# A message-passing kernel: additions in PSUM, the relu shared by two engines, 101 copied groups

## The chip, the core and the metric

The kernel runs on one core of a Trainium2 chip. A core has five engines with a queue of instructions each, worked off in order: TensorE (PE: matrix products, results in the accumulator memory PSUM), VectorE (DVE), ScalarE (ACT), GpSimd (POOL, which here issues the indirect gathers) and SyncE (SP, which issues plain DMAs). Engines wait for each other by semaphores. The metric is the time of one execution on the device, in microseconds (us), and the number that counts is the median of several.

## The reference

One layer of a graph network with a residual and a layer norm: 12500 nodes of 64 features, 200000 edges of 32 features, sorted by destination.

```python
msg_in = concatenate([nodes[row], nodes[col], edge_features], axis=-1)   # 64 + 64 + 32
messages = relu(msg_in @ mW1 + mb1) @ mW2 + mb2                          # hidden 128
aggregated = segment_sum(messages, col, num_segments=12500)
upd = relu(concatenate([nodes, aggregated]) @ uW1 + ub1) @ uW2 + ub2
out = layernorm(nodes + upd)
```

All is float32. `row` is the source of an edge (random), `col` its destination (sorted).

## The kernel before

**Tables.** The product of the first weight with a concatenation is a sum of products. The kernel first writes table A, the product of every node with the source part of `mW1`, to DRAM, and table B, the same for the destination part with the bias. An edge then needs one row of A (by its source) and one of B (by its destination).

**Tiles, steps and groups.** 128 edges are a tile; 1563 tiles. A step `s` has 6 tiles (261 steps), a super-step 12 tiles, two steps. In the loop over steps, `gather` (L209) has POOL fetch 128 rows of A by an indirect DMA, one instruction a tile, into one of 9 row buffers. `edge_part` (L367) has PE multiply the edge features and a one-hot of the destination within a window of 32 nodes with the edge weights and the rows of B, into a PSUM accumulator `pc` of two banks. `node_part` adds the gathered rows: DVE writes `h = pc + xg` (L394, 128x768), ACT then applies the relu to `h` in place (L395). `collect` (L424, L427) has PE sum the hidden rows `h` into the nodes of the window with a one-hot `sel`, written by DVE in `select` (L235, L237, L243) once a super-step, in even steps. `collect(s - 1)` and `edge_part(s + 1)` are issued in step s. Every 7 or 8 steps a period of nodes is closed (L441, L442), updated (L464 to L480) and normed (L486 to L510). The first ten steps gather rows of x and multiply them on PE, since A is not there yet.

**Copied groups.** In 96 of the steps (16, 19, 21, 24, ..., two in five), POOL gathers only 4 of the 6 tiles. The rows of the last two come from a copy of x that lies transposed in SBUF (`xtop`, `xbot`): for each of 128 columns an instruction copies one column for each of two tiles at once into `xc`, and PE multiplies `xc` with the weight (L370) into the same accumulator. Of the 128 columns, ACT copies 64 (`singly`, L338) and DVE 64 (`joined`, L345). In such a step the addition is 128x512 (L390) with its relu (L391), and the relu of the copied tiles reads PSUM (L392). Where a column lies comes from the edge's source number: `addresses` (L315) loads a chunk of up to 8 columns, two addresses each, from the list `col_a` into registers of the engine, and the copies behind it use them. `portion(s, total, unit)` says which columns of which group are due in step s; two copy buffers hold the groups under way.

**Order.** The order of each queue is the order of the Python loop over steps, written by hand: node part, a third or a half of DVE's copies, the norm stages of an older period, `collect(s - 1)`, `select` of the next super-step with a third of the copies between its operations, a chunk of table B (until step 50), the update, `edge_part(s + 1)`, the rest of DVE's copies, and last ACT's copies. The last lines of the loop body:

```python
            rest(s)
            joined(s, 2 if j == 0 and g + 1 < NSUP else 1, 3 if j == 0 and g + 1 < NSUP else 2)
            singly(s, 0, 1)
```

A buffer of gathered rows is free again once the addition of its step is done; `pc` (two buffers, shared with the products of table B, the update and the residual) once the last reader is done.

Of the kernel before, what the change touches and what calls it, by code (L numbers as in the profile page):

```python
# [24 lines left out]
SUB = 6  # L25
SUP = 12
NSUP = -(-NT // SUP)
NTP = NSUP * SUP
EPAD = NTP * P
NSUB = -(-NT // SUB)  # L30
# [39 lines left out]
XBASE = 8320  # L70
U8 = mybir.dt.uint8
YBASE = XBASE + 4 * XCOLS
FIRST, GAPS = 16, (3, 2)
COPIED = []
while FIRST + sum(GAPS) * (len(COPIED) // len(GAPS)) + sum(GAPS[:len(COPIED) % len(GAPS)]) < NSUB - 6:
    COPIED.append(FIRST + sum(GAPS) * (len(COPIED) // len(GAPS)) + sum(GAPS[:len(COPIED) % len(GAPS)]))
RNDS = -(-len(COPIED) // len(GAPS))
LAST = 4 * (N - 1)
ACTS, CHUNK = 64, 8


def updates():
# [19 lines left out]
def gnn_kernel(ctx: ExitStack, tc: tile.TileContext, x1T, x, eT, e_rows, src, src_row, dst, dst_row, wlist, wrow, wnext, whalf,  # L102
# [24 lines left out]
    nc = tc.nc  # L127
    const = ctx.enter_context(tc.tile_pool(name="const", bufs=1))
# [12 lines left out]
    wint = const.tile([1, len(LISTS)], I32, name="wint")  # L141
    past = const.tile([1, 1], F32, name="past")

    cols = const.tile([RNDS * len(GAPS), 2 * P], I32, name="cols")
    col_a = const.tile([RNDS * len(GAPS), P, 2], I32, name="col_a")
    w1b = const.tile([P, DH], F32, name="w1b")
    b1 = const.tile([P, DH], F32, name="b1")

# [43 lines left out]
    def tiles(s):  # L192
        return range(s * SUB, min((s + 1) * SUB, NT))
# [20 lines left out]
    with tc.tile_pool(name="sup", bufs=2) as sup, tc.tile_pool(name="work", bufs=2) as work, tc.manual_schedule():  # L214
# [13 lines left out]
        def select(g, at=None):  # L228


            nt = min(SUP, NT - g * SUP)
            l = L[g]
            c = WIN + SUP // 2 * (g % 2)
            node = cps[:, c:c + SUP // 2]
            nc.vector.tensor_scalar(node, wh[:, g * SUP // 2:(g + 1) * SUP // 2], pidx, None, op0=ALU.add)  # L235
            for r in ([slice(0, P)] if g > 2 else [slice(q, q + WIN) for q in SK]):
                nc.vector.tensor_tensor(l[r], l[r].bitcast(I32),  # L237
                                        node[r].unsqueeze(2).broadcast_to([r.stop - r.start, SUP // 2, P]),
                                        op=ALU.is_equal)
            if at is not None:  # L240
                joined(at, 1, 3)
            s = sup.tile([P, SUP, WIN], F32, name="sel")
            nc.vector.tensor_tensor(s[:, :nt], slot.unsqueeze(1).broadcast_to([P, nt, WIN]),  # L243
                                    drc[:, g * SUP:g * SUP + nt].unsqueeze(2).broadcast_to([P, nt, WIN]),
                                    op=ALU.is_equal)
            S[g] = s

        def counts(g):

            SB[g] = S[g].bitcast(BF).rearrange("p k (w h) -> p k w h", h=2)  # L250
# [36 lines left out]

        def columns_list():

            for r in range(len(GAPS)):  # L290
                v = src_row[:, ((FIRST + sum(GAPS[:r])) * SUB + SUB - 2) * P:]
                nc.sync.dma_start(cols[r * RNDS:(r + 1) * RNDS],
                                  bass.AP(v.tensor, v.offset, [[sum(GAPS) * SUB * P, RNDS], [1, 2 * P]]))
            cv = cols.rearrange("k (b e) -> k b e", b=2)
            for b, base in enumerate((XBASE, YBASE)):
                nc.vector.tensor_scalar(col_a[:, :, b], cv[:, b], 4.0, float(base), op0=ALU.mult, op1=ALU.add)

        x8, y8 = xtop.bitcast(U8), xbot.bitcast(U8)

        def portion(s, total, unit):  # L300

            rate, found = sum(GAPS) / len(GAPS), []
            begin = min(c - 2 - (j + 1) * rate for j, c in enumerate(COPIED[:len(GAPS)]))
            for j, c in enumerate(COPIED):
                lo, hi = (min(-(-int(total * (s + d - begin - j * rate) / rate * 16 + 0.5) // (16 * unit)) * unit, total) for d in (0, 1))
                lo = max(lo, 0)
                if lo < hi:
                    if c not in xc:
                        xc[c] = work.tile([P, P], F32, name="xc")
                    found.append((xc[c], j % len(GAPS) * RNDS + j // len(GAPS), lo, hi))  # L310
            return found

        def addresses(k, a, m, engine):

            _, v = nc.values_load_multi_w_load_instructions(  # L315
                col_a.rearrange("k e b -> k (e b)")[k:k + 1, 2 * a:2 * m], engines=[engine], min_val=XBASE,
                max_val=YBASE + LAST, skip_runtime_bounds_check_because="sources are node numbers")
            v = [w.with_bounds(min_val=base, max_val=base + LAST, guaranteed_mod_val=0, out_of_modulus=4)
                 for w, base in zip(v, (XBASE, YBASE) * (m - a))]
            return [(e, x8[:, bass.ds(v[2 * (e - a)] - XBASE, 4)], y8[:, bass.ds(v[2 * (e - a) + 1] - YBASE, 4)])  # L320
                    for e in range(a, m)]

        def share(todo, part, of):

            n = -(-len(todo) // of)
            todo = todo[part * n:part * n + n]
            while todo:
                o, k, a = todo[0]
                m = min(len([t for t in todo if t[1] == k]), CHUNK // 2)
                todo = todo[m:]  # L330
                yield o, k, a, a + 2 * m

        def singly(s, part, of):

            todo = [(o, k, e) for o, k, lo, hi in portion(s, ACTS, 2) for e in range(lo, hi, 2)]
            for o, k, a, m in share(todo, part, of):
                for e, top, bot in addresses(k, a, m, ET.Activation):
                    nc.scalar.activation(o[:, e:e + 1], top.bitcast(F32), AF.Identity, bias=bot.bitcast(F32))  # L338

        def joined(s, part, of):  # L340

            todo = [(o, k, ACTS + e) for o, k, lo, hi in portion(s, P - ACTS, 2) for e in range(lo, hi, 2)]
            for o, k, a, m in share(todo, part, of):
                for e, top, bot in addresses(k, a, m, ET.DVE):
                    nc.vector.tensor_tensor(o[:, e:e + 1].bitcast(I32), top.bitcast(I32), bot.bitcast(I32),  # L345
                                            op=ALU.bitwise_or)
# [26 lines left out]
        def node_part(s):  # L373

            n = len(tiles(s))
            pc = pcs.pop(s)
            h = work.tile([P, 2, SUB // 2, DH], F32, name="h")
            if s < XG:
                xt = xs.pop(s)
                for i in range(n):  # L380
                    k, b = divmod(i, 2)
                    q = 64 * b
                    nc.tensor.matmul(pc[:, b, k, :], xt[q:q + 64, k, :], w1a[q:q + 64], start=False,
                                     stop=i + 2 >= n)
                nc.scalar.activation(h, pc, AF.Relu)
            else:
                a = xg.pop(s)[0].rearrange("p (b k) f -> p b k f", b=2)
                if s in COPIED:
                    m = SUB // 2 - 1
                    nc.vector.tensor_tensor(h[:, :, :m], pc[:, :, :m], a[:, :, :m], op=ALU.add)  # L390
                    nc.scalar.activation(h[:, :, :m], h[:, :, :m], AF.Relu)  # L391
                    nc.scalar.activation(h[:, :, m:], pc[:, :, m:], AF.Relu)  # L392
                for b, m in parts(n) if s not in COPIED else []:
                    nc.vector.tensor_tensor(h[:, b, :m], pc[:, b, :m], a[:, b, :m], op=ALU.add)  # L394
                    nc.scalar.activation(h[:, b, :m], h[:, b, :m], AF.Relu)  # L395
            hs[s] = h

        def opened(u):
# [354 lines left out]
        for s in range(last + 2):  # L753
            g, j = divmod(s, SUP // SUB)
# [20 lines left out]
                    stage(K - 2)  # L775
            if s < NSUB:
                node_part(s)
                joined(s, 0, 3 if j == 0 and g + 1 < NSUP else 2)
            for stage, n in ((evacuate, 2), (statistics, 3), (deviation, 4), (norm, 5)):
                if earlier(n) is not None:  # L780
                    stage(earlier(n))
# [42 lines left out]
    with tc.If(flag > 0), tc.tile_pool(name="gen", bufs=1) as up:  # L824
# [28 lines left out]
        with tc.For_i(0, NT, 1) as t:  # L853
# [26 lines left out]
            pc = psum.tile([P, DH], F32, name="pcg", tag="pc")  # L880
# [4 lines left out]
            h = up.tile([P, DH], F32, name="hg")  # L885
# [6 lines left out]
            m = up.tile([P, 1], F32, name="m")  # L892
# [22 lines left out]
        with tc.For_i(0, NB, 1) as c:  # L915
# [24 lines left out]
            o = up.tile([P, D], F32, name="o")  # L940
# [49 lines left out]
```

## Time and profile before

| | |
|---|---|
| runs | 1737.85, 1738.25, 1740.77 us; median 1738.25 |
| profiled execution | 1741.33 us, span of the records 1739.5 us, 46406 instructions |
| POOL | 1298.0 us busy, 1371 gathers |
| ACT | 1469.7 us busy |
| DVE | 1057.8 us busy |
| PE | 1460.8 us busy, granted clock 0.579 of full speed |
| DMA | 192.43 MB, 111 GB/s over the span |

The page of the profile has the busy time of each engine, the chain of work that ended last, and groups of instructions by source line, each with its count, busy time and mean duration, and the idle time of the engine in front of it with what ended that. "Issue" means that the engine waited for nothing that the profile shows: for POOL the time to issue a gather, for DVE and ACT mostly a load of addresses, which is no busy time. A busy engine need not be the one that bounds, nor an engine with gaps be free.

### The profile page before, as it was taken

The page shows a single profiled execution, that of the slowest core. Times are in us where ns is not written, and L with a number is a line of the kernel's source. Part 1 is how long each engine was busy: PE and PEld are TensorE (multiplying, and loading weights), DVE is VectorE, ACT ScalarE, POOL GpSimd, SP SyncE. Part 2 cuts the span into 40 slices and gives each one's busy share as a digit, 9 for nine tenths or more (in the row PEclk, how much of TensorE's full clock was granted, in tenths as well). Part 3 has the DMA queues.
Part 4 walks back from the last instruction along what each step waited for, and adds up shares of the span by engine and source line. Part 5 has one row for each costly group of instructions (what it writes and reads, how often), then busy time and mean ns, then how long its engine had stood idle before and what let it go on. Part 6 is the DMA issues. An engine that isn't in the chain of part 4 may idle for free.

```text
span 1739.5 us, 46406 instructions
## 1 busy us (share of the span) xinstructions
PE 1460.8 (84%) x9620; PEld 1259.4 (72%) x9620; DVE 1057.8 (61%) x7327; ACT 1469.7 (84%) x6712; POOL 1298.0 (75%) x1380
## 2 busy tenths in 40 slices
PE   2696788888988888888987889999888878899997
PEld 2586778877777778677876777778766767777776
DVE  1527666666666666566666666666666666666642
ACT  0277989999999898899899899999999899999941
POOL 7777777777777777777777777777777777777773
PEclk8585555555555555555566555555556566565655
DMA  8773444433333333333343344343344444444442
GB/s 212 205 175 100 129 110 115 116 95 99 99 102 92 96 96 96 96 104 94 98 108 104 105 107 105 103 108 103 105 110 110 106 107 110 107 108 110 108 113 61
DMA packets 207588, 192.43 MB, mean 111 GB/s; under 512 B 57511, under 2 KB 173409, under 8 KB 207313
## 3 DMA queue, kind: packets, MB, share of 16 engines
q0 software_dynamic: 43872, 87.97, 20.6%
q1 hardware_dynamic: 148896, 92.54, 19.4%
q10 hardware_dynamic: 14546, 8.93, 1.8%
q8 instruction: 91, 1.49, 0.4%
q14 instruction: 183, 1.50, 0.3%
HBM read 171.53 MB, written 17.76 MB: 109 GB/s over the span
## 4 chain that ended last, share of the span: by engine, by line
POOL 37%; issue 23%; DMA 14%; DVE 13%; PE 8%; DVEq 3%; ACT 1%; SPq 1%; ACTq 0%; POOLq 0%
POOL xg L209 37%; DMA xg<-tab_a,src_s 10%; DVE xc L345 6%; DVE h L394 3%; PE sums L427 3%; DVEq L315 3%; PE pc L367 2%; DVE l L237 2%; DMA tab_a<-tb 1%; ACT xc L338 1%; DVE h L390 1%; PE pu L464 1%; DMA w1b<-in_mW 1%; PE pu L465 1%; PE py L478 0%
## 5 line engine op out<-in xcount | busy, mean ns | idle before, releaser
L209 POOL DMA_INDIRECT xg<-tab_a,src_s x1311 | 1239.5, 945 | 399.7 <-issue 368.6
L338 ACT ACTIVATE xc<-xtop,xbot 128x1 f32 x6144 | 1166.8, 280 | 43.0 <-issue 32.8
L345 DVE TENSOR_TENSOR xc<-xtop,xbot 128x1 int32 x6144 | 537.2, 154 | 416.4 <-issue 402.0
L427 PE MATMUL sums<-sel,h 128*128 128x32 f32 x3126 | 643.6, 373 | 21.9 <-ACT h L395 15.9
L427 PEld LDWEIGHTS sums<-sel,h 128*128 128x128 f32 x3126 | 610.0, 296 | 41.3 <-ACT h L395 17.4
L367 PE MATMUL pc<-rhs,l 64*128 64x128 f32 x3126 | 424.5, 418 | 172.3 <-DVE h L394 112.0
L367 PEld LDWEIGHTS pc<-rhs,l 64*128 64x128 f32 x3126 | 352.2, 296 | 235.6 <-DVE h L394 135.8
L395 ACT ACTIVATE h<-h 128x768 f32<-128x768 f32 x156 | 129.6, 831 | 108.8 <-DVE h L394 104.8
L394 DVE TENSOR_TENSOR h<-pc,xg 128x768 f32<-128x768 f32 x156 | 148.0, 949 | 118.5 <-DMA xg<-tab_a,src_s 76.5
L237 DVE TENSOR_TENSOR l<-l,cps 128x768 f32<-128x768 int32 (+1 forms) x134 | 127.8, 953 | 21.2 <-DMA l<-in_dst_row 16.6
L424 PEld LDWEIGHTS <-one 128*1 128x1 bf16 x1563 | 57.5, 83 | 62.4 <-issue 53.4
L424 PE MATMUL cnt<-sel,one 128*1 128x32 bf16 x1563 | 91.8, 187 | 0.9 <-issue 0.6
L390 DVE TENSOR_TENSOR h<-pc,xg 128x512 f32<-128x512 f32 x96 | 66.1, 688 | 30.2 <-PE pc L370 13.5
L243 DVE TENSOR_TENSOR sel<-cps,drc 128x384 f32<-128x384 f32 x131 | 71.6, 547 | 10.9 <-PE sums L427 10.9
L370 PE MATMUL pc<-w1a,xc 64*128 64x128 f32 x384 | 75.7, 400 | 0.0
L209 POOL DMA_INDIRECT xg<-in_x,src_s x60 | 57.4, 957 | 19.1 <-issue 17.7
L464 PE MATMUL pu<-xw,uz 128*128 128x448 f32 (+1 forms) x68 | 59.9, 982 | 13.3 <-DVE h L394 13.3
L370 PEld LDWEIGHTS pc<-w1a,xc 64*128 64x128 f32 x384 | 67.7, 315 | 0.0
L391 ACT ACTIVATE h<-h 128x512 f32<-128x512 f32 x96 | 59.3, 617 | 8.1 <-DVE h L390 7.7
L583 ACT COPY tb<-pb 128x512 f32<-128x512 f32 (+1 forms) x13 | 7.4, 569 | 59.0 <-DMA tab_a<-tb 26.8
L465 PE MATMUL pu<-sums_s,w2u 128*128 128x448 f32 (+1 forms) x68 | 53.4, 888 | 0.0
L478 PE MATMUL py<-ux,xw 128*128 128x64 f32 x268 | 49.3, 343 | 2.4 <-DVE h L394 2.4
(104 smaller groups left out, 784.8 us busy)
## 6 DMA issues: line engine op xcount, KB each, us to landing
l<-in_dst_row SPq DMA_DIRECT2D x262, 96.0 KB
l<-in_eT SPq DMA_DIRECT2D x262, 96.0 KB
xg<-tab_a,src_s POOLq DMA_INDIRECT x1311
rhs<-tab_b SPq DMA_DIRECT2D x361, 32.0 KB
tab_b<-tb SPq DMA_DIRECT2D x13, 512.0 KB
rhs<-tab_b SPq DMA_DIRECT2D x387, 16.0 KB
tab_a<-tb ACTq DMA_DIRECT2D x12, 512.0 KB
out<-y SPq DMA_DIRECT2D x33, 128.0 KB
```

The source lines that it names most:

```text
L209: nc.gpsimd.indirect_dma_start(out=a[:, i, :] if s < XG else a[:, i // 2, i % 2, :], out_offset=None, in_=A[:, :] if s >= XG else x[:, :], ...
L237: nc.vector.tensor_tensor(l[r], l[r].bitcast(I32), node[r].unsqueeze(2).broadcast_to([r.stop - r.start, SUP // 2, P]), op=ALU.is_equal)
L338: nc.scalar.activation(o[:, e:e + 1], top.bitcast(F32), AF.Identity, bias=bot.bitcast(F32))
L345: nc.vector.tensor_tensor(o[:, e:e + 1].bitcast(I32), top.bitcast(I32), bot.bitcast(I32), op=ALU.bitwise_or)
L367: nc.tensor.matmul(pc[:, b, k, :], L[g][q:q + 64, m, :], rhs[g % 2][q:q + 64, w, :], start=s >= XG or k == 0, stop=s >= XG and not copied)
L370: nc.tensor.matmul(pc[:, b, k, :], xc[s][q:q + 64], w1a[q:q + 64], start=False, stop=True)
L390: nc.vector.tensor_tensor(h[:, :, :m], pc[:, :, :m], a[:, :, :m], op=ALU.add)
L394: nc.vector.tensor_tensor(h[:, b, :m], pc[:, b, :m], a[:, b, :m], op=ALU.add)
L395: nc.scalar.activation(h[:, b, :m], h[:, b, :m], AF.Relu)
L424: nc.tensor.matmul(pn[:, bass.ds(ws[i], WIN)], one, SB[g][:, k0 + i, :, 1], start=False, stop=ends and i == n - 1)
L427: nc.tensor.matmul(ps[:, bass.ds(ws[i], WIN)], h[:, i % 2, i // 2, :], S[g][:, k0 + i, :], start=False, stop=ends and i == n - 1)
L464: nc.tensor.matmul(pu, uz, xw[u % 2][:, :n], start=True, stop=False)
```

## The change

- **Addition in PSUM.** `node_part` adds the gathered rows into `pc` in place. Then ACT applies the relu to the first bank (`h[:, 0]`, 128x384) and DVE to the second (`h[:, 1]`), both from PSUM into `h`. This holds for all full steps from the tenth on, copied or not.
- **Address loads.** The function `joined` gives way to `quota` (the columns of a step), `fetch` (load addresses for up to n columns) and `join` (copy them). A fetch of 8 columns (6 in a copied step) stands between the addition and DVE's relu, one of 4 behind the relu, one of 8 behind L237 (the select's second operation) and one of 4 behind the select's last operation. What is left goes in chunks of 8 at the end of the step.
- **Groups.** 101 groups instead of 96, at steps 16, 18, 20, 23, 25, ... 254, from a progress function: 0.43 groups a step at the start, 0.41 at the end. ACT copies 66 columns, DVE 62. Three copy buffers for two.
- **List of addresses.** `col_a` holds the addresses of the last two tiles of every step, where before it held those of the copied steps alone.

```diff
-FIRST, GAPS = 16, (3, 2)
+BEGIN, FINAL = 11, 255
+RATES = 0.43, 0.41
+SWING = 0.0
+
+def progress(s, early=0.0):
+    s = max(s + 1 - BEGIN, 0)
+    return s * (RATES[0] + (RATES[1] - RATES[0]) * s / (2 * NSUB)) + (early if s else 0.0)
+
 COPIED = []
-while FIRST + sum(GAPS) * (len(COPIED) // len(GAPS)) + sum(GAPS[:len(COPIED) % len(GAPS)]) < NSUB - 6:
-    COPIED.append(FIRST + sum(GAPS) * (len(COPIED) // len(GAPS)) + sum(GAPS[:len(COPIED) % len(GAPS)]))
+for s in range(NSUB):
+    while min(progress(s), progress(s, -SWING if s % 2 else SWING)) >= len(COPIED) + 1 and s + 3 < FINAL:
+        COPIED.append(s + 3)
-ACTS, CHUNK = 64, 8
+ACTS, CHUNK = 66, 8
...
-    cols = const.tile([RNDS * len(GAPS), 2 * P], I32, name="cols")
-    col_a = const.tile([RNDS * len(GAPS), P, 2], I32, name="col_a")
+    col_a = const.tile([P, 2, P, 2], I32, name="col_a")
...
             if at is not None:
-                joined(at, 1, 3)
+                join(fetch(quota(at), 8))
             s = sup.tile([P, SUP, WIN], F32, name="sel")
             nc.vector.tensor_tensor(s[:, :nt], slot.unsqueeze(1).broadcast_to([P, nt, WIN]),
...
             S[g] = s
+            if at is not None:
+                join(fetch(quota(at), 4))
...
-        def portion(s, total, unit):
+        def portion(s, total, early=(0.0, 0.0)):
...
-                lo, hi = (min(-(-int(total * (s + d - begin - j * rate) / rate * 16 + 0.5) // (16 * unit)) * unit, total) for d in (0, 1))
-                lo = max(lo, 0)
+                lo, hi = (min(max(int((progress(s + d, early[d + 1]) - j) * total / 2 + 1e-6) * 2, 0), total) for d in (-1, 0))
                 if lo < hi:
                     if c not in xc:
-                        xc[c] = work.tile([P, P], F32, name="xc")
+                        xc[c] = work.tile([P, P], F32, name="xc", bufs=3)
...
-        def joined(s, part, of):
-            todo = [(o, k, ACTS + e) for o, k, lo, hi in portion(s, P - ACTS, 2) for e in range(lo, hi, 2)]
-            for o, k, a, m in share(todo, part, of):
-                for e, top, bot in addresses(k, a, m, ET.DVE):
-                    nc.vector.tensor_tensor(o[:, e:e + 1].bitcast(I32), top.bitcast(I32), bot.bitcast(I32),
-                                            op=ALU.bitwise_or)
+        def quota(s):
+            if s not in quotas:
+                quotas[s] = [(o, k, ACTS + e) for o, k, lo, hi in portion(s, P - ACTS) for e in range(lo, hi, 2)]
+            return quotas[s]
+
+        def fetch(todo, n):
+            ready = []
+            while todo and n:
+                o, k, a = todo[0]
+                m = min(len([t for t in todo if t[1] == k]), n // 2)
+                del todo[:m]
+                n -= 2 * m
+                ready += [(o, *x) for x in addresses(k, a, a + 2 * m, ET.DVE)]
+            return ready
+
+        def join(ready):
+            for o, e, top, bot in ready:
+                nc.vector.tensor_tensor(o[:, e:e + 1].bitcast(I32), top.bitcast(I32), bot.bitcast(I32),
+                                        op=ALU.bitwise_or)
...
-                if s in COPIED:
-                    m = SUB // 2 - 1
-                    nc.vector.tensor_tensor(h[:, :, :m], pc[:, :, :m], a[:, :, :m], op=ALU.add)
-                    nc.scalar.activation(h[:, :, :m], h[:, :, :m], AF.Relu)
-                    nc.scalar.activation(h[:, :, m:], pc[:, :, m:], AF.Relu)
-                for b, m in parts(n) if s not in COPIED else []:
-                    nc.vector.tensor_tensor(h[:, b, :m], pc[:, b, :m], a[:, b, :m], op=ALU.add)
-                    nc.scalar.activation(h[:, b, :m], h[:, b, :m], AF.Relu)
+                m = SUB // 2 - (s in COPIED)
+                todo = quota(s)
+                if n == SUB:
+                    nc.vector.tensor_tensor(pc[:, :, :m], pc[:, :, :m], a[:, :, :m], op=ALU.add)
+                    ready = fetch(todo, 6 if s in COPIED else 8)
+                    nc.scalar.activation(h[:, 0], pc[:, 0], AF.Relu)
+                    nc.vector.tensor_scalar(h[:, 1], pc[:, 1], 0.0, None, op0=ALU.max)
+                    join(ready + fetch(todo, 4))
+                else:
+                    for b, m in parts(n):
+                        nc.vector.tensor_tensor(h[:, b, :m], pc[:, b, :m], a[:, b, :m], op=ALU.add)
+                        nc.scalar.activation(h[:, b, :m], h[:, b, :m], AF.Relu)
             hs[s] = h
...
                 node_part(s)
-                joined(s, 0, 3 if j == 0 and g + 1 < NSUP else 2)
...
             rest(s)
-            joined(s, 2 if j == 0 and g + 1 < NSUP else 1, 3 if j == 0 and g + 1 < NSUP else 2)
+            while s < NSUB and quota(s):
+                join(fetch(quota(s), CHUNK))
             singly(s, 0, 1)
```

More of the change, by code (lines that the diff above doesn't have):

```diff
@@ L72 @@
 YBASE = XBASE + 4 * XCOLS
-FIRST, GAPS = 16, (3, 2)
+BEGIN, FINAL = 11, 255
[4 more added lines that the diff above has]
+    return s * (RATES[0] + (RATES[1] - RATES[0]) * s / (2 * NSUB)) + (early if s else 0.0)
 COPIED = []
-while FIRST + sum(GAPS) * (len(COPIED) // len(GAPS)) + sum(GAPS[:len(COPIED) % len(GAPS)]) < NSUB - 6:
-    COPIED.append(FIRST + sum(GAPS) * (len(COPIED) // len(GAPS)) + sum(GAPS[:len(COPIED) % len(GAPS)]))
-RNDS = -(-len(COPIED) // len(GAPS))
+for s in range(NSUB):
+    while min(progress(s), progress(s, -SWING if s % 2 else SWING)) >= len(COPIED) + 1 and s + 3 < FINAL:
+        COPIED.append(s + 3)
 LAST = 4 * (N - 1)
-ACTS, CHUNK = 64, 8
+ACTS, CHUNK = 66, 8
 def updates():
@@ L288, in columns_list @@
         def columns_list():
[L290 to L296, printed above, removed]
+            cols = work.tile([P, 2, 2, P], I32, name="cols", tag="tb")
+            for r in range(2):
+                n = min(P, NSUB - 1 - r * P)
+                v = src_row[:, (r * P * SUB + SUB - 2) * P:]
+                nc.sync.dma_start(cols[:n, r].rearrange("k b e -> k (b e)"),
+                                  bass.AP(v.tensor, v.offset, [[SUB * P, n], [1, 2 * P]]))
+                for b, base in enumerate((XBASE, YBASE)):
+                    nc.vector.tensor_scalar(col_a[:n, r, :, b], cols[:n, r, b], 4.0, float(base), op0=ALU.mult, op1=ALU.add)
         x8, y8 = xtop.bitcast(U8), xbot.bitcast(U8)
-        def portion(s, total, unit):
-            rate, found = sum(GAPS) / len(GAPS), []
-            begin = min(c - 2 - (j + 1) * rate for j, c in enumerate(COPIED[:len(GAPS)]))
+        def portion(s, total, early=(0.0, 0.0)):
+            found = []
             for j, c in enumerate(COPIED):
-                lo, hi = (min(-(-int(total * (s + d - begin - j * rate) / rate * 16 + 0.5) // (16 * unit)) * unit, total) for d in (0, 1))
-                lo = max(lo, 0)
+                lo, hi = (min(max(int((progress(s + d, early[d + 1]) - j) * total / 2 + 1e-6) * 2, 0), total) for d in (-1, 0))
                 if lo < hi:
                     if c not in xc:
-                        xc[c] = work.tile([P, P], F32, name="xc")
-                    found.append((xc[c], j % len(GAPS) * RNDS + j // len(GAPS), lo, hi))
+                        xc[c] = work.tile([P, P], F32, name="xc", bufs=3)
+                    found.append((xc[c], c, lo, hi))
             return found
@@ L315, in addresses @@
             _, v = nc.values_load_multi_w_load_instructions(
-                col_a.rearrange("k e b -> k (e b)")[k:k + 1, 2 * a:2 * m], engines=[engine], min_val=XBASE,
+                col_a[k % P:k % P + 1, k // P].rearrange("k e b -> k (e b)")[:, 2 * a:2 * m], engines=[engine], min_val=XBASE,
                 max_val=YBASE + LAST, skip_runtime_bounds_check_because="sources are node numbers")
@@ L333, in singly @@
         def singly(s, part, of):
-            todo = [(o, k, e) for o, k, lo, hi in portion(s, ACTS, 2) for e in range(lo, hi, 2)]
+            todo = [(o, k, e) for o, k, lo, hi in portion(s, ACTS) for e in range(lo, hi, 2)]
             for o, k, a, m in share(todo, part, of):
@@ L338, in singly @@
                     nc.scalar.activation(o[:, e:e + 1], top.bitcast(F32), AF.Identity, bias=bot.bitcast(F32))
-        def joined(s, part, of):
-            todo = [(o, k, ACTS + e) for o, k, lo, hi in portion(s, P - ACTS, 2) for e in range(lo, hi, 2)]
-            for o, k, a, m in share(todo, part, of):
-                for e, top, bot in addresses(k, a, m, ET.DVE):
-                    nc.vector.tensor_tensor(o[:, e:e + 1].bitcast(I32), top.bitcast(I32), bot.bitcast(I32),
-                                            op=ALU.bitwise_or)
+        def quota(s):
[15 more added lines that the diff above has]
+                                        op=ALU.bitwise_or)
+        quotas = {}
         xc = {}
```

## The prediction

> **What bounds the kernel now.** I read the page's busy rows and chain first, then the table of waits, then the time at which each step's gather and addition start, and last the timeline of a stretch in which no data is waited for. The rows of the page:
>
> ```profile
> PE 1460.8 (84%) x9620; PEld 1259.4 (72%) x9620; DVE 1057.8 (61%) x7327; ACT 1469.7 (84%) x6712; POOL 1298.0 (75%) x1380
> POOL 37%; issue 23%; DMA 14%; DVE 13%; PE 8%; DVEq 3%; ACT 1%; SPq 1%; ACTq 0%; POOLq 0%
> L209 POOL DMA_INDIRECT xg<-tab_a,src_s x1311 | 1239.5, 945 | 399.7 <-issue 368.6
> L338 ACT ACTIVATE xc<-xtop,xbot 128x1 f32 x6144 | 1166.8, 280 | 43.0 <-issue 32.8
> L345 DVE TENSOR_TENSOR xc<-xtop,xbot 128x1 int32 x6144 | 537.2, 154 | 416.4 <-issue 402.0
> ```
>
> POOL looks 75% busy, but before nearly every gather stands the 0.30 us that it needs to issue it. The waits:
>
> ```profile
> DVE xc L345 <- issue: 402.0, 862, 1.6
> POOL xg L209 <- issue: 386.2, 1267, 0.3
> ...
> DVE h L394 <- DMA xg<-tab_a,src_s: 76.5, 53, 7.0
> ```
>
> So POOL never stops: 1371 gathers from 2.9 to 1717.5 us, 1.249 us from one start to the next (0.945 + 0.30). What follows the last gather takes 22 us. The second thing to see is the third row: additions wait for data. By the start times of L394/L390, the addition of a step starts 29 us behind its last gather at steps 10 to 34, 6 us behind at steps 60 to 84, and 2.5 to 3.3 us from step 85 on. The step engines thus have a faster pace than POOL, catch up by step 70, and then stand still for data. The pace that they can do is visible only before that: 6.16 us a step over steps 16 to 50 (162.87 to 372.15 us; table B is still built there) and 5.68 over steps 52 to 70 (384.53 to 486.74). POOL's is 6.5. In that stretch the vector engine waits for no data:
>
> ```profile
> 402.25 0.96 DVE L394 TENSOR_TENSOR h<-pc,xg 128x768 f32<-128x768 f32 x1
> 403.49 0.67 DVE L345 TENSOR_TENSOR xc<-xtop,xbot 128x1 int32 x8 [0.29 <-issue]
> 404.73 0.54 DVE L345 TENSOR_TENSOR xc<-xtop,xbot 128x1 int32 x6 [0.57 <-issue]
> 406.16 0.65 DVE L345 TENSOR_TENSOR xc<-xtop,xbot 128x1 int32 x8 [0.88 <-issue]
> 407.13 0.42 DVE L345 TENSOR_TENSOR xc<-xtop,xbot 128x1 int32 x4 [0.33 <-issue]
> 407.54 0.69 DVE L390 TENSOR_TENSOR h<-pc,xg 128x512 f32<-128x512 f32 x1
> ```
>
> The step is filled by short copies and by address loads. A load of 16 addresses takes 1.12 us, of 12 0.87, of 8 0.61, of 4 0.35 (medians of L315 on DVE; 1.05 for 16 on ACT); it starts up to four copies ahead of the engine, but **behind an addition that waits it starts only with it** (25 ns after, in the median of all 79 such additions of L394).
>
> **Five more copied groups.** 101 for 96: 10 gathers fewer, 10 x 1.249 = 12.5 us off POOL's path. That is the whole gain that can be had while POOL stays the bound, and it needs the step engines at no more than about 6.35 us a step from the start.
>
> **Where the copies lie.** ACT gets 66 columns of 101 groups, 6666 for 6144, at 0.186 us from start to start: 27.4 a step, 5.1 us, against 4.7. DVE gets 6262 at 0.070, 25.8 a step, as before. The progress rule only moves them towards the start (0.43 groups a step falling to 0.41, against 0.40). The third copy buffer lets a group begin early; a wait for one was no row before, so it is costed at nothing.
>
> **The relu on ACT.** One instruction of 128x384 from PSUM for one of 128x768 (0.83), or for 128x512 and 128x256 (0.62 + 0.36). The rows from PSUM give 0.36 for 256 and 0.80 for 768 columns, so 0.47, of which the next instruction overlaps 0.09. But the address load behind it now has nothing to hide under: where the relu waited, the first copy began 1.18 us after its start in before (mean of 41), and that is the load's time, which a shorter relu doesn't shorten. ACT's step: 5.1 copies + 0.25 for closing, update and norm (1.9 us for each of 33 updates) + 0.38 = 5.7 where the relu finds ACT late, and 1.15 in the place of 0.38, **6.5, where ACT has waited for it**.
>
> **The addition in PSUM.** Its source rows are unchanged (0.957 for 768, 0.688 for 512). No row writes this much into PSUM from DVE. Bounds: 0.05 less (no reason excludes a gain), and 0.1 more, as the 128x6 operation that writes PSUM (L235) takes 0.218 against 0.15 to 0.17 for such small ones into SBUF. I take no change.
>
> **The relu on DVE.** A copy of 128x512 out of PSUM takes 0.689 and an operation of 128x384 0.547, so 0.55. In the instruction order of the changed program it carries one wait: for ACT's relu of the same step. So the two relus do not run beside each other. The chain is addition, ACT's relu, DVE's relu, and everything behind the last on DVE (the copies, the next select, the next addition) stands behind ACT's queue. Before, DVE never waited for ACT's relu.
>
> **A pair of steps on DVE**, in the new order. Both: addition 0.96, hand-over 0.03, ACT's relu 0.47, back 0.05; the load of 16 (1.12) hides under this. At 1.51 the DVE relu starts, and the load of 8 behind it only then: 0.61 + 0.09, first copy at 2.22; twelve copies to 3.06. The even step goes on with L235 (0.26), L237 and a load of 16 behind it (1.22 to the first copy, as in before), 8 copies 0.56, select 0.5 (its load of 8 starts early and is hidden), 4 copies, a last load of 4 or 8 partly hidden and some 0.45 from its first copy to the next addition: 6.4. The odd step has a load of 16 that leaves 0.9 open, 8 copies, a load of 12 that leaves 0.65, 6 copies and the same end: 5.7. Copied steps have a shorter addition (0.27 less in 4 of 10), and more columns left for the end; the two about cancel. Statistics and norms are 0.26 a step. **DVE alone: 6.3 us a step.** The loads cost some 1.2 a step in the place of 1.6 (402.0 us over 250 steps): 0.4 is won, and 0.55 (relu) and 0.55 (its wait) are paid.
>
> **The two together.** After the long even step (6.4 + 0.26) ACT has waited, so its next turn is 6.5, longer than DVE's 5.95 for the odd one: (6.66 + 6.5) / 2 = 6.6. The closing and norm work falls at times where there is slack, so I take 6.5, between 6.3 and 6.6.
>
> **Sum.** The first 34 copied steps were 0.45 us slower than later ones (6.16 against 5.68, table B); kept, 6.95 each: addition of step 50 at 162.9 + 236 = 399, still in front of POOL's need of the buffer. Steps 50 to 253: 203 x 6.5 = 1320. Six steps without copies at about 5: 30. From the addition of step 259 to the end 23.4 as in before (1716.12 to 1739.5). Together 1772 of span; the profiled execution was 1.8 us over its span, and 3.1 above the median of the runs shown (1741.33 against 1738.25), so about 1770; **I say 1768**, since some slack of the last steps returns. Each 0.1 us of step is 20 us.
>
> **PE.** Its accumulators are freed by the DVE relu, 1.1 us after the addition's end, and the 65 waits of L367 on L394 (135.8 us) get longer, up to 70 us in all. It is one step ahead of DVE, so I cost this at nothing; without that cover it is the 70.
>
> **The rivals.**
> 1. POOL stays the bound. Either the odd and even steps even out so that DVE's 6.3 or a little less holds, or the load passes the waiting relu. For the latter the Trainium skill has a rule (Advanced Engine Details and Errata, Sequencer and Instruction Queues): an instruction waits for its semaphore in the engine's queue while the sequencer reads on. By that the load would run during the wait. In rows: the first copy 0.2 us earlier on DVE and 0.75 on ACT, (6.45 + 5.75) / 2 = 6.1 a step, under POOL's 6.44. The 79 waiting additions speak against it; the load started 25 ns after them. Either way 1738.25 - 12.5 = 1725.8. Chance 0.30, of which the rule 0.08.
> 2. ACT's wait or PE's is dearer: the addition 0.1 longer, the coupling full, PE's 70 us partly on the path. 6.7 a step: 1768 + 40 = 1808. For it: PE is 84% busy. Chance 0.13.
> 3. Pace and POOL meet, and the change gives back what it takes, 1735 to 1741. Chance 0.05.
>
> It decides at 6.35 us a step: below, the change is worth its 12.5 us; at 6.38 nothing.
>
> **How the numbers follow.** Forecast 0.52, 1745 to 1795, slower. Rival 2 is slower too: slower 0.65, faster 0.30, same 0.05, where same is within 0.2%, about what three runs that lie 2.9 us apart can tell. The range reaches down to rival 1's 1725.8 and up to 1800, leaving out most of rival 2 and a little below.
>
> **What would show it.** Right: DVE's relu starts right behind ACT's end in nearly every step and waits for it some 0.5 us each; ACT waits for the addition in even steps and leaves 0.77 between relu and copy; POOL has waits for its buffers (released by DVE) in the second half, and additions lag their gathers by tens of us at the end. Wrong: POOL's pitch 1.249 throughout with 1361 gathers, and additions still waiting for data after step 150.

## The result

The changed kernel takes 1838.47 us (median of 4 runs, 1835.49 to 1838.70) against 1738.05 us (1737.54 to 1740.77): a ratio of 1.0569, with a 95% interval of 1.0556 to 1.0581. It is 100 us slower. The forecast of 1768 us had the direction, and the time lies outside its range of 1725 to 1800.

The page of the changed kernel (L218 is the gather, L348 and L370 the copies of ACT and DVE, L418 the addition, L420 and L421 the relus of ACT and DVE, L325 the loads of addresses):

```profile
PE 1549.1 (84%) x9640; PEld 1334.0 (73%) x9640; DVE 1175.5 (64%) x7697; ACT 1478.9 (81%) x7138; POOL 1290.4 (70%) x1370
...
ACT 25%; DVE 21%; POOL 17%; issue 14%; DMA 8%; PE 7%; ACTq 6%; DVEq 2%; SPq 0%; POOLq 0%
...
L421 DVE TENSOR_SCALAR h<-pc 128x384 f32<-128x384 f32 x250 | 139.4, 557 | 234.8 <-ACT h L420 228.7
L418 DVE TENSOR_TENSOR pc<-pc,xg 128x768 f32<-128x768 f32 (+1 forms) x250 | 214.1, 856 | 30.3 <-PE pc L394 10.0
L420 ACT ACTIVATE h<-pc 128x384 f32<-128x384 f32 x250 | 120.2, 481 | 132.6 <-DVE pc L418 131.2
```

ACT has 9 us more work than before. DVE has 118 us more, but is busy for 64% of the span; two of the runs below carry the same work without most of the loss. The chain of work that ended last was POOL's before; now ACT and DVE lead it and POOL holds 17%. The table of waits says why (who waited for whom: us in total, times, longest):

```profile
...
DVE xc L370 <- issue: 274.9, 640, 1.2
DVE h L421 <- ACT h L420: 228.7, 241, 7.3
ACT h L420 <- DVE pc L418: 131.2, 116, 7.3
...
ACT xc L348 <- issue: 92.9, 163, 2.0
POOL xg L218 <- DVE pc L418: 82.4, 73, 2.8
```

DVE waited for ACT's relu in 241 of 250 steps. POOL, which never waited for a buffer before, now waits for the addition that frees one; each of the 73 waits holds the 0.3 us that it takes to issue a gather anyway, so some 60 of the 82.4 us are new. By the start times, in means over 25 steps, the addition of a step begins 51 to 54 us behind the end of its last gather from step 35 to the end (in the kernel before 2.5 to 3.3 us, from step 85 on). That is as far as nine row buffers reach: nine steps of 6.7 us, less the 6.5 us in which POOL issues one step's gathers. Open loads, the time in which an engine stands for a load of addresses (the rows with "issue"), fell on DVE from 402.0 to 274.9 us and rose on ACT from 32.8 to 92.9.

Two steps of the timeline show the mechanism: step 125, an odd one, whose addition starts at 912.37, and step 126, an even one, at 917.90 (start, duration, in brackets the idle time before and who ended it). DVE:

```profile
912.37 0.97 DVE L418 TENSOR_TENSOR pc<-pc,xg 128x768 f32<-128x768 f32 x1
913.96 0.56 DVE L421 TENSOR_SCALAR h<-pc 128x384 f32<-128x384 f32 x1 [0.62 <-ACT h L420]
914.66 0.95 DVE L370 TENSOR_TENSOR xc<-xtop,xbot 128x1 int32 x12
916.27 0.65 DVE L370 TENSOR_TENSOR xc<-xtop,xbot 128x1 int32 x8 [0.66 <-issue]
917.48 0.51 DVE L370 TENSOR_TENSOR xc<-xtop,xbot 128x1 int32 x6 [0.56 <-issue]
917.90 0.69 DVE L418 TENSOR_TENSOR pc<-pc,xg 128x512 f32<-128x512 f32 x1
920.26 0.56 DVE L421 TENSOR_SCALAR h<-pc 128x384 f32<-128x384 f32 x1 [1.66 <-ACT h L420]
...
925.85 0.97 DVE L418 TENSOR_TENSOR pc<-pc,xg 128x768 f32<-128x768 f32 x1 [0.20 <-DMA xg<-tab_a,src_s]
```

and ACT in the same stretch:

```profile
913.43 0.49 ACT L420 ACTIVATE h<-pc 128x384 f32<-128x384 f32 x1 [0.26 <-DVE pc L418]
914.56 5.29 ACT L348 ACTIVATE xc<-xtop,xbot 128x1 f32 x28 [0.63 <-issue]
919.76 0.47 ACT L420 ACTIVATE h<-pc 128x384 f32<-128x384 f32 x1
920.13 0.35 ACT L517 COPY y<-py 128x256 f32<-128x256 f32 x1
920.38 5.30 ACT L348 ACTIVATE xc<-xtop,xbot 128x1 f32 x28
926.85 0.49 ACT L420 ACTIVATE h<-pc 128x384 f32<-128x384 f32 x1 [1.17 <-DVE pc L418]
```

In the first step ACT waited for the addition; its load of addresses starts only with the relu and leaves 0.63 us open behind it. So its 28 copies end 0.6 us later; the next addition is done at 918.6 and finds ACT still copying until 919.8, and DVE stands for 1.66 us. Then DVE's own longer, even step makes ACT wait again (1.17 us at 926.85). The mean over all steps from 52 to 149: an even step (from addition to addition) 7.26 us, an odd one 6.08; ACT's relu begins 0.58 us after the end of the addition in even steps, 0.15 in odd ones, and ACT idled 0.14 and 0.68 us in front of it.

### The profile page after: what moved, and what is told of

Same layout as the page of the kernel before. It is cut to its first block, busy times and chain, and to the rows that moved or that the text cites. A ratio compares the mean times of both kernels' runs of the same rounds, so it can differ in the third digit from the quotient of the medians.

```text
span 1836.9 us, 47402 instructions
## 1 busy us (share of the span) xinstructions
PE 1549.1 (84%) x9640; PEld 1334.0 (73%) x9640; DVE 1175.5 (64%) x7697; ACT 1478.9 (81%) x7138; POOL 1290.4 (70%) x1370
## 4 chain that ended last, share of the span: by engine, by line
ACT 25%; DVE 21%; POOL 17%; issue 14%; DMA 8%; PE 7%; ACTq 6%; DVEq 2%; SPq 0%; POOLq 0%
ACT xc L348 20%; POOL xg L218 17%; DVE xc L370 7%; ACTq L325 6%; DMA xg<-tab_a,src_s 5%; DVE pc L418 4%; ACT h L420 3%; DVE l L246 3%; DVE h L421 2%; PE sums L458 2%; DVEq L325 2%; PE pc L394 2%; DMA tab_a<-tb 1%; DVE sel L252 1%; DMA xtop<-in_x1T 1%
## 5 line engine op out<-in xcount | busy, mean ns | idle before, releaser
L218 POOL DMA_INDIRECT xg<-tab_a,src_s x1301 | 1231.7, 947 | 462.9 <-issue 355.0
L348 ACT ACTIVATE xc<-xtop,xbot 128x1 f32 x6666 | 1265.9, 280 | 102.9 <-issue 92.9
L370 DVE TENSOR_TENSOR xc<-xtop,xbot 128x1 int32 x6262 | 525.0, 153 | 289.5 <-issue 274.9
L458 PE MATMUL sums<-sel,h 128*128 128x32 f32 x3126 | 677.9, 384 | 34.7 <-ACT h L420 34.5
L458 PEld LDWEIGHTS sums<-sel,h 128*128 128x128 f32 x3126 | 640.3, 308 | 58.9 <-ACT h L420 39.3
L394 PE MATMUL pc<-rhs,l 64*128 64x128 f32 x3126 | 448.3, 429 | 184.3 <-DMA l<-in_eT 67.5
L421 DVE TENSOR_SCALAR h<-pc 128x384 f32<-128x384 f32 x250 | 139.4, 557 | 234.8 <-ACT h L420 228.7
L418 DVE TENSOR_TENSOR pc<-pc,xg 128x768 f32<-128x768 f32 (+1 forms) x250 | 214.1, 856 | 30.3 <-PE pc L394 10.0
L420 ACT ACTIVATE h<-pc 128x384 f32<-128x384 f32 x250 | 120.2, 481 | 132.6 <-DVE pc L418 131.2
L218 POOL DMA_INDIRECT xg<-in_x,src_s x60 | 57.6, 960 | 19.2 <-issue 18.0
L509 PEld LDWEIGHTS py<-ux,xw 128*128 128x128 f32 x268 | 54.2, 299 | 7.3 <-issue 4.4
L511 PE MATMUL py<-u,hTu 128*128 128x64 f32 x268 | 59.6, 397 | 0.0
L511 PEld LDWEIGHTS py<-u,hTu 128*128 128x128 f32 x268 | 56.5, 310 | 0.0
```

Source lines behind the costliest of these rows:

```text
L218: nc.gpsimd.indirect_dma_start(out=a[:, i, :] if s < XG else a[:, i // 2, i % 2, :], out_offset=None, in_=A[:, :] if s >= XG else x[:, :], ...
L394: nc.tensor.matmul(pc[:, b, k, :], L[g][q:q + 64, m, :], rhs[g % 2][q:q + 64, w, :], start=s >= XG or k == 0, stop=s >= XG and not copied)
L418: nc.vector.tensor_tensor(pc[:, :, :m], pc[:, :, :m], a[:, :, :m], op=ALU.add)
L420: nc.scalar.activation(h[:, 0], pc[:, 0], AF.Relu)
L421: nc.vector.tensor_scalar(h[:, 1], pc[:, 1], 0.0, None, op0=ALU.max)
L458: nc.tensor.matmul(ps[:, bass.ds(ws[i], WIN)], h[:, i % 2, i // 2, :], S[g][:, k0 + i, :], start=False, stop=ends and i == n - 1)
```

## Experiments

For each: the ratio is to the kernel before on the same chip; its median was between 1737.9 and 1739.3 us on the chips of this table, so the times may be compared too. The pace is the mean distance of the additions over steps 52 to 149 and 150 to 251, worked out from their start times; 6.44 us is POOL's with 101 groups. POOL's floor with them is the time before less ten gathers, 1726 us. The lag is the time from the end of a step's last gather to the start of its addition, in means over 25 steps.

| run | us | ratio, 95% | pace |
|---|---|---|---|
| the change | 1838.5 | 1.0569 (1.0556 to 1.0581) | 6.67, 6.79 |
| whole relu on ACT | 1730.5 | 0.9948 (0.9931 to 0.9964) | 6.22, 6.32 |
| DVE's relu first | 1748.4 | 1.0059 (1.0042 to 1.0075) | 6.27, 6.45 |
| before, 101 groups | 1725.7 | 0.9922 (0.9905 to 0.9938) | 6.12, then POOL's |
| the change, 96 groups | 1787.1 | 1.0281 (1.0255 to 1.0306) | 6.41, 6.62 |
| two accumulators | 1728.6 | 0.9947 (0.9929 to 0.9965) | 6.19, 6.34 |
| loads alone | 1725.5 | 0.9924 (0.9907 to 0.9940) | 6.15, then POOL's |
| before, 106 groups | 1774.4 | 1.0204 (1.0187 to 1.0221) | 6.46, 6.57 |
| ACT's load early | 1791.3 | 1.0303 (1.0286 to 1.0320) | 6.47, 6.61 |
| before, 103 groups | 1731.5 | 0.9959 (0.9946 to 0.9972) | 6.24, 6.36 |
| two accumulators, 103 groups | 1748.9 | 1.0059 (1.0042 to 1.0076) | 6.28, 6.41 |

The theory: DVE's relu, by its wait for ACT's relu of the same step, ties the two queues together, and that costs the time. Rivals: the addition in PSUM, the new places of the loads, DVE's additional relu as work, more columns to copy.

**The whole relu on ACT.**

```diff
-                    nc.scalar.activation(h[:, 0], pc[:, 0], AF.Relu)
-                    nc.vector.tensor_scalar(h[:, 1], pc[:, 1], 0.0, None, op0=ALU.max)
+                    nc.scalar.activation(h, pc, AF.Relu)
```

> One edit to the changed kernel: both banks' relu on ACT (one 128x768 from PSUM), none on DVE; the addition in PSUM, the order of the address loads, 101 groups and three buffers stay. Theory (the relu on DVE and its wait for ACT's relu of the same step cost the time: DVE gets 0.56 more work and up to 0.6 us of wait a step, and ACT idles in odd steps): DVE never waits for ACT, pace under POOL's 6.44 us a step, POOL's pitch back at 1.25 us, 1726 to 1735 us. Rival (the addition in PSUM, which holds the accumulator longer, or the new places of the loads): still above 1800.

1730.5 us: 108 us of the 113 that lie between the change and POOL's floor of 1726 are gone with one line. Addition in PSUM, places of the loads and number of groups are the same, so none of them costs more than a few us once DVE has no relu. This run takes away DVE's relu together with its wait, so it doesn't tell the work from the wait; the next one does.

**DVE's relu first.** The split stays; the two instructions change places.

```diff
-                    nc.scalar.activation(h[:, 0], pc[:, 0], AF.Relu)
                     nc.vector.tensor_scalar(h[:, 1], pc[:, 1], 0.0, None, op0=ALU.max)
+                    nc.scalar.activation(h[:, 0], pc[:, 0], AF.Relu)
```

> One edit to the changed kernel: the two relu instructions change places, so that DVE's comes right behind the addition and ACT's waits for it; the work on each engine is the same to the instruction. Theory: it is the wait on ACT that costs, not the 0.56 us of DVE's relu; DVE's pace falls from 6.73 to about 6.0 us a step, ACT's wait of 0.55 more a step fits under POOL's pace, 1726 to 1745 us. Rival (DVE's additional work of 0.56 us a step costs it): above 1790.

1748.4 us, 3 above the expected span and 90 below the change, with the same work on every engine. The waits of this run (L420 is DVE's relu here, L421 ACT's):

```profile
...
DVE xc L370 <- issue: 282.2, 710, 1.3
ACT xc L348 <- issue: 74.8, 140, 1.4
DVE h L420 <- DVE pc L418: 71.9, 230, 1.0
...
ACT h L421 <- DVE h L420: 56.4, 56, 6.6
```

DVE's relu waits for nothing but DVE's own addition. So it is the direction of the wait that cost 90 us. My reading of why, which no run isolates: ACT has 5 us of copies that can run late; DVE has in its queue the next addition, for which ACT waits in turn.

**The kernel before with 101 groups.** Into the kernel before go the progress rule, 66 columns on ACT, the long list and the third buffer; `joined`, the addition into SBUF and the relu stay.

```diff
-FIRST, GAPS = 16, (3, 2)
+BEGIN, FINAL = 11, 255
+RATES = 0.43, 0.41
...
-ACTS, CHUNK = 64, 8
+ACTS, CHUNK = 66, 8
...
-                        xc[c] = work.tile([P, P], F32, name="xc")
+                        xc[c] = work.tile([P, P], F32, name="xc", bufs=3)
```

> The kernel before with 101 groups, the progress rule, 66 columns on ACT, the long address list and three copy buffers; addition into SBUF, relu on ACT and places of the loads as before. Theory: ACT's pace is 27.4 copies x 0.186 + 0.77 + 0.25 = 6.1 us a step, DVE's about 5.7, POOL stays the bound: 1726 us (10 gathers x 1.249 less). Rival (more columns to copy cost the time): above 1780.

1725.7 us, the floor as worked out: 10 gathers x 1.249 us. POOL's pitch is 1.250 us in the mean, and additions have caught up with the gathers by step 160 (lag 3.8 us over steps 160 to 184). ACT is close to its limit here: 98.6% busy from 400 to 1600 us, against 87.9% in the changed kernel. This kernel beats both.

**The change with 96 groups.**

```diff
-RATES = 0.43, 0.41
-ACTS, CHUNK = 66, 8
+RATES = 0.4, 0.4
+ACTS, CHUNK = 64, 8
```

> The changed kernel with a rate of 0.40 throughout, 96 groups and 64 columns on ACT, as many copies as before; all else as changed. Theory: the lockstep stays, ACT's part shrinks by 0.35 us a step: 6.5 to 6.65 us a step, 1785 to 1820 us, still slower than before. Rival (more columns to copy): 1738 us.

1787.1 us: as many copies as in the kernel before, and still 2.8% or 49 us slower. The other 51 us of the change come with the five more groups, but only in company with the wait; without it they cost nothing, as the run before shows.

**Two accumulators.** Why does DVE's relu wait for ACT's at all? They read different banks and write different halves of `h`. With `h` as two tiles the built program (the list of instructions and waits of each engine) still has the wait, which was not run; with the accumulator as two tiles it has it no more. So the program sets the wait, and it goes with the accumulator being one PSUM tile.

```diff
-            pc = psum.tile([P, 2, 4, DH], F32, name="pc")[:, :, :SUB // 2]
+            pc = [psum.tile([P, 4, DH], F32, name=f"pc{b}")[:, :SUB // 2] for b in range(2)]
...
-                    nc.vector.tensor_tensor(pc[:, :, :m], pc[:, :, :m], a[:, :, :m], op=ALU.add)
+                    for b in range(2):
+                        nc.vector.tensor_tensor(pc[b][:, :m], pc[b][:, :m], a[:, b, :m], op=ALU.add)
```

> The changed kernel with the accumulator of a step as two PSUM tiles of one bank each (the addition as two instructions of 128x384, the products of table B, the update and the residual moved to match): then DVE's relu waits for its own addition alone, and the two relus run beside each other as the change says. Theory (the wait for ACT's relu cost): DVE's and ACT's pace about 6.1 to 6.25 us a step, POOL the bound or nearly, 1726 to 1745 us, under the 1748 of the exchanged relus. Rival (DVE's second relu costs by its work): above 1770.

1728.6 us, 110 below the change. The same two relus on the same engines, and a second addition a step on top:

```profile
...
DVE xc L370 <- issue: 281.4, 700, 1.8
PEld pc L394 <- issue: 118.4, 81, 3.9
DVE h L423 <- DVE pc L420: 88.3, 226, 1.0
ACT xc L348 <- issue: 65.6, 119, 2.3
ACT h L422 <- DVE pc L420: 59.3, 54, 6.8
```

L423, DVE's relu, waits for L420, DVE's addition, alone. The 0.56 us of work are carried within 3 us of the floor; the wait was the loss. The data didn't need it: the two relus overlapped in 127 of 250 steps, in 79 by more than 0.2 us, and in these DVE's took 557 ns, as in the mean of all. One thing more came with this edit: ACT's relu waits for the first half of the addition alone, and in 121 steps it began before the second half had ended. How much of the 20 us between this run and DVE's relu first is due to that was not tried.

**The loads alone.** The changed kernel with addition and relu as before.

```diff
-                    nc.vector.tensor_tensor(pc[:, :, :m], pc[:, :, :m], a[:, :, :m], op=ALU.add)
+                    nc.vector.tensor_tensor(h[:, :, :m], pc[:, :, :m], a[:, :, :m], op=ALU.add)
                     ready = fetch(todo, 6 if s in COPIED else 8)
-                    nc.scalar.activation(h[:, 0], pc[:, 0], AF.Relu)
-                    nc.vector.tensor_scalar(h[:, 1], pc[:, 1], 0.0, None, op0=ALU.max)
+                    nc.scalar.activation(h[:, :, :m], h[:, :, :m], AF.Relu)
+                    if s in COPIED:
+                        nc.scalar.activation(h[:, :, m:], pc[:, :, m:], AF.Relu)
```

> The changed kernel with the addition into SBUF and the whole relu on ACT, as before; the places of the loads, 101 groups and three buffers stay. Two theories on why the relu on ACT (first run) kept a lag of 13 us at its end where the kernel before with 101 groups had caught up by step 160. By the addition in PSUM: here the lag is gone by step 160, 1726 us. By the places of the loads: the lag stays 10 to 20 us at steps 235 on, 1728 to 1735 us.

1725.5 us, the floor too; but the lag was 14 us over steps 160 to 184 and gone only by step 235. Neither theory is met as written. The addition of step 150 began at 998.3 us in the kernel before with 101 groups, at 1011.6 here, and at 1023.3 with the whole relu on ACT. Of these 25 us, some 12 lie between the last two, that is, with the addition into PSUM and the relu that then reads PSUM; the other 13 lie between the first two, of which 5 were there at step 16 already (next point). The new places win nothing once DVE has no relu of its own. Open loads of DVE, here and in the kernel before with 101 groups:

```profile
DVE xc L370 <- issue: 485.4, 721, 1.9
```

```profile
DVE xc L353 <- issue: 396.0, 858, 1.6
```

Fewer waits, and longer in total: in this program, without DVE's relu, two loads stand directly behind each other.

**The kernel before, once more**, for its start.

> The kernel before, once more, for its start. The addition of step 16 began at 162.9 us in its profile and at 169.5 to 175.1 in the five others. If that is the new list and start of the copies: 163 again. If it varies from run to run: anywhere to 170.

1739.25 us in its one run. Step 16 began at 166.9 us, 4 later than in the first profile; in the kernels with 101 to 106 groups it was 163.5 to 175.8. So at least 4 us of the 12 that the changed kernel lost before step 16 vary from run to run. The list and the early start of the copies are in the run with two accumulators too, which began at 165.4, so they are not the rest. What it is stays open.

**106 groups in the kernel before**, 62 columns on ACT.

```diff
-RATES = 0.43, 0.41
-ACTS, CHUNK = 66, 8
+RATES = 0.445, 0.435
+ACTS, CHUNK = 62, 8
```

> The kernel before with 106 groups (rates 0.445 to 0.435) and 62 columns on ACT, 66 on DVE; else as the run with 101 groups. Theory: ACT's part stays as with 101 groups (27.3 copies a step), DVE's grows by 3.2 copies and their loads, 0.3 us, to about 6.0; POOL stays the bound: 20 gathers less than before, 1738 - 25 = 1713 to 1720 us. If DVE becomes the bound instead: 1725 to 1745.

1774.4 us: a miss, above both spans. The pace is 6.46 to 6.57, over POOL's 6.39. I had added only DVE's copies and loads; its open loads grew from 396.0 us, with 101 groups, to 472.0, and PE's waits for the addition (L375 on L402) from 63.1 to 107.1. Which of these carried it was not tried.

**ACT's load early.** The changed kernel, with the first load of ACT's columns put ahead of ACT's relu; the wait of DVE's relu stays.

```diff
                     ready = fetch(todo, 6 if s in COPIED else 8)
+                    begin(s)          # loads the addresses of ACT's first chunk
                     nc.scalar.activation(h[:, 0], pc[:, 0], AF.Relu)
```

> The changed kernel with the first address load of ACT's columns ahead of ACT's relu instead of behind it; DVE's relu still waits for ACT's. It isolates one term: the 0.7 us that ACT stood between its relu and its first copy in steps where it had waited for the addition, by which DVE waits longer in the next step. Theory (this coupling is a part of its own): even steps lose most of their 0.58 us of wait, pace 6.35 to 6.5 us a step instead of 6.73, 1745 to 1785 us. Rival (only DVE's own chain of addition, ACT's relu and DVE's relu counts): within 10 us of 1838.

1791.3 us: 47 us of the loss were this one load, though 6 us fewer than expected at least. ACT's relu in even steps now begins 0.21 us after the addition (0.28 from step 150 on) instead of 0.58, and the waits are

```profile
ACT h L430 <- DVE pc L427: 188.9, 170, 8.5
DVE h L431 <- ACT h L430: 178.6, 240, 6.5
```

ACT now idles 0.39 us in front of its relu in even steps and 0.92 in odd ones. So what is left, 6.90 us for an even step and 6.05 for an odd one, 6.47 in the mean, is in the main DVE's own chain of addition, ACT's relu and its own.

**103 groups**, in the kernel before (rates 0.437 to 0.421) and with two accumulators and ACT's early load.

> The kernel before with 103 groups (rates 0.437 to 0.421), 66 columns on ACT. With 101 it had caught up with POOL by step 160, with 0.28 us a step to spare; a group more costs ACT 66 x 0.186 = 12.3 us and takes 2.5 off POOL, so two more should use up what is left: 1721 us if they fit, 1722 to 1735 if ACT becomes the bound.

> Two accumulators (the relus beside each other), ACT's first load ahead of its relu, and 103 groups. ACT's open loads were 65.6 us in the run with two accumulators and 101 groups, whose lag at the end was 4.5 us; 40 us of them gone pay for two groups more: 1721 to 1728 us. If the loads were no bound there: 1730 to 1750.

1731.5 and 1748.9 us, both over the 101 groups of the same kernel. At the end the additions lag 24.5 and 29.9 us behind the gathers, where they lagged 3.1 and 4.5 with 101. The step engines are the bound again: 101 groups are about what either order can carry. What the early load is worth with two accumulators isn't told by this run, as two groups came with it (pace 6.28 for 6.19); it didn't pay for them. These three kernels (ACT's load early and the two with 103 groups) were first run on a chip on which everything took about 2500 us: 2478.9, 2518.3 and 2459.9 us, and 2538.9 the kernel before. All three were ahead of the kernel before there, in another order than here; nothing of that is used, and why is not known.

## Why the prediction was wrong

*POOL's path, 12.5 us for ten gathers.* Right: 1725.7 us in the kernel before with 101 groups, 1725.8 forecast.

*The two relus do not run beside each other.* Right, and the cause of the loss. The coupling by which ACT's turn, once it has waited, is 6.5 us was right too: from ACT's relu in an odd step to that in the even step behind it, 6.51 us passed over steps 52 to 149 and 6.48 over 150 to 251. DVE's relu takes 0.557 us (0.55 forecast), ACT's 0.48 (0.47), the hand-overs 0.10 from the addition to ACT's relu (0.03 forecast) and 0.03 back (0.05).

*A load behind a waiting instruction starts only with it.* Right. In all 240 steps in which a load stood directly behind DVE's waiting relu, it began 13 to 24 ns after the relu, never during the wait; the first copy followed 0.70 us after the relu's start (0.71 forecast). The rule of the Trainium skill (Advanced Engine Details and Errata, Sequencer and Instruction Queues), by which, as I read it, the sequencer reads on meanwhile, does not describe this wait; the measurement decides.

*The addition in PSUM, taken as no change.* Right in its duration (0.97 for 128x768), but perhaps not free: the whole relu on ACT has a pace 0.07 us above the loads alone, which differ in where the addition writes and in where the relu reads.

*The pair of steps on DVE.* From DVE's relu to the next addition I had 6.4 - 1.51 + 0.26 = 5.15 in the even step and 4.45 in the odd; measured were 5.32 (steps 52 to 149) and 5.55 (150 to 251), and 4.56 and 4.53. The even step was sized 0.2 to 0.4 too short, 0.1 to 0.2 a step. The growth has a cause that the 0.26 for statistics and norms hid by being a mean over all steps. Periods are not closed every 7 or 8 steps: that is the mean too. By the start times of the statistics (L525), two closings lie 19 steps apart at step 51 and 3 or 4 around step 245. So this work took 0.11 us of an even step over steps 52 to 149 and 0.41 over 150 to 251.

*The two together: "The closing and norm work falls at times where there is slack, so I take 6.5".* This step failed, in both its parts. The longer turn, from ACT's relu in an even step to that in the odd one, was to be 6.66 us; it was 6.83 over steps 52 to 149 and 7.10 over 150 to 251, since DVE's even step was too short in the sum, and the norm work lengthened it instead of falling into slack. And the working gave 6.6, which I rounded down by an argument that no row carried. The pace was 6.67 over steps 52 to 149 and 6.79 after, 6.73 from 50 to 254: half of 6.83 and 6.51, the two turns, is 6.67, and half of 7.10 and 6.48 is 6.79. With 20 us of time for 0.1 us, the 0.23 are 47 us of the miss: some 16 by the rounding (6.58 to 6.5), the rest by the even step.

*The wait of DVE's relu, 0.55 a step without the coupling.* It was 0.67 in odd steps, where ACT's relu was nearly on time, and 1.09 in even ones, where it came late: 0.91 in the mean (228.7 us over 250 steps). The loads came out as said, 1.1 us a step (274.9) for 1.2.

*PE, taken at nothing.* Right: additions waited for PE five times, 16.5 us in all.

*The rest of the sum.* Steps 16 to 50 took 234.6 us (236 forecast), but by luck: the pace behind them was 0.17 above the 6.5, and they were only 0.23 above that pace, not 0.45. The end took 23.3 us (23.4). The last five steps, 254 to 259, took 30.2 us, where I had six for 30. The start was no term: step 16 began at 175.1 us, not 162.9, 12 us. So 12 + 54 (204 steps at 6.73 for 203 at 6.5) - 1 is the 65 us between the forecast span of 1772 and the 1836.9 measured. By this sum the change would have been worth its 12.5 us up to 6.28 us a step, and nothing at 6.34; the 6.35 and 6.38 of the prediction don't come out of it.

*Rival 2*, the dearer coupling at 6.7 a step with 1808 us, had the pace; I gave it 0.13, and its time lacked the start. Of its three reasons one came: the coupling was full. The addition was 0.01 us longer, not 0.1, and PE's 70 us did not come, so its pace was in part luck.

*What would show it.* Nearly all of it was there: the waits of L421, ACT idle with an open load behind its relu (0.6 us, 0.77 forecast), POOL waiting for the addition. POOL's waits came from step 33 on, not in the second half. ACT's wait was named for the even steps; it stood in front of the relu of the odd steps (0.68 us, against 0.14), which is where the working had put it, behind the long even step.

## What to carry to other kernels

Before an operation is split between two engines, see in the built program whether the halves wait for each other: a tile shared by them can set a wait that the data doesn't need, and here two tiles removed it. A wait put into the queue of an engine that feeds the other one took the slack out of both queues here; with the wait in the other queue most of the loss was gone. When the sum of a chain through two engines comes out over the bound, it isn't rounded down for slack that no row shows; and work that comes in bunches, as the norms do, is not spread over all steps by its mean.

## What was unexpected of the hardware

Nothing in the single durations. One chip took 2539 us for the kernel before where the others took 1738. In the kernel with 103 groups, the copies of ACT (0.279 us against 0.278) and its loads of 16 addresses (1.04 us on both chips) were as long as elsewhere; the time went into gaps. ACT's open loads were 337 us against 12, DVE's 566 against 412, and POOL waited for additions at 184 gathers, 677 us in all, on the other chip at none beyond its 0.3 us of issue. The cause is not known.
